# Delta rule's second pass: copies behind their updates, GpSimd's product at the head of a step, and the feed-forward branch shifted between the passes

## The chip, the cores and the metric

The kernel runs on one core of one Trainium2 chip. The metric is the device time of one execution in microseconds (us). The engines of the core work side by side, each through its own queue in program order: PE (TensorE, matrix products into PSUM), DVE (VectorE), ACT (ScalarE), POOL (GpSimd) and SP, which issues transfers.

## What is computed

The reference is a network of four layers on 4 x 1024 tokens of width 128, all in fp32; each layer adds an attention branch and a feed-forward branch to the tokens. Only the fourth layer bears on the change. Its attention branch is a delta rule: for each of 16 heads a state S of 8 x 8 is carried along the 1024 tokens. Its other branch is a feed-forward layer with a sine.

```python
# attention branch (delta rule), per head
v_new = (v_t - k_t @ S) * b_t
S = S + outer(k_t, v_new)
o_t = q_t @ S

# other branch
hidden = x @ W1 + b1
imag = w_imag * sin(theta + hidden * 0.1)
act = relu(hidden + (cos(theta) * w_real + sin(theta) * w_imag) * imag * 0.1)
out = act @ W2 + b2
```

## The kernel before, in words

`_delta_rule` cuts the 1024 tokens of each head into CH = 32 chunks of N = 32 tokens and works on all chunks at once, so that one step is one token of every chunk. The 128 partitions hold 4 batches x 16 heads x 2 halves of the value columns. There are three stages.

1. **First pass** (L1981 to L1994, 32 steps): every chunk starts from unit and zero states (`sm`, `sn` in PSUM), and what comes out are the linear map and the offset of each chunk.
2. **Scan** (L2006 to L2018, 31 steps on DVE): chunk after chunk, the true state at each chunk's start.
3. **Second pass** (L2028 to L2043, 32 steps and one more for the last state): the recurrence is run again from the true states, and the outputs are formed. The chunks form two halves of 16 chunks, one in `sm`, one in `sn`; both are worked in every step.

In the second pass, `differ` (L1941 to L1951) does one half of a step: on DVE `pro` (state times key, L1941), `dd` (a sum over d, L1944), a subtraction (L1946) and `u` (L1951). PE then builds the new state in PSUM by two additions (L1927): an identity matrix times `hist`, which is a copy of the old state in SBUF, then minus `u`. The copy from PSUM to `hist` is ACT's (L1955). POOL multiplies a complete `hist` with the query (`dprod`, L2041), and DVE sums that product into the output (`dvo`, L2025).

The order on PE, DVE, ACT and POOL is the order in which the program issues the instructions (the layer is under a hand-written schedule). In the order before, a step i issues for half 0: `pro`, the copy to `hist` (which was due before `pro`'s update), `dd`, the subtraction, `u`; then `output(i-2)`; then the same for half 1; then POOL's product of the state that this step copied. So the product issued at the end of one step is summed in the middle of the next one. `hist` and `dprod` have two buffers each.

The other branch is the generator `_waves` (L2047). It has 32 items (8 stretches of 512 tokens x 4 blocks of hidden units), worked in a pipeline of parts that alternate:

- **part A**: `close` of item n-3 (DVE L2110, every fourth item), `leave` of item n-2 (PE L2106), `sine` of item n-1: a clamp on DVE (L2094), then the sine on ACT (L2095);
- **part B**: `rest` of item n-1 (DVE L2099, ACT L2100), `enter` of item n (PE L2083, three activations on ACT, L2085, L2087, L2088), `fold` of item n (POOL L2091).

The clamp of an item thus waits for the `fold` of the part B before. `_layer3` (L2187) interleaves the two: `_delta_rule` yields 32 times in the first pass (n = 0 to 31, at the end of each step), 31 times in the scan (n = 32 to 62) and twice in each step of the second pass (from n = 63 on: an odd n lies between the halves, behind `output`; an even n lies at the end of the step). At some of these yields one part of `_waves` is issued. L2205 says at which: every odd n in the first pass (16 parts), two of three in the scan (21 parts), and every odd n in the second pass (33 parts): one part in the middle of every step, A and B in turn.

After that `_delta_out` (L2123) normalises and projects the outputs.

Of the kernel before, what the change touches and what calls it, by code (L numbers as in the profile page):

```python
# [16 lines left out]
ALU = mybir.AluOpType  # L17
AX = mybir.AxisListType
# [202 lines left out]
def _bc(ap, axis, n):  # L221

    ap = ap.unsqueeze(axis)
    shape = list(ap.shape)
    shape[axis] = n
    return ap.to_broadcast(shape)
# [1592 lines left out]
def _delta_rule(k, s, wl):  # L1819
# [6 lines left out]
    nc = k.nc  # L1826
    CH = 32
    N = L // CH
# [9 lines left out]
    room = lambda t: s.room(t).rearrange("p (c v d) -> p c v d", v=4, d=8)  # L1838
# [83 lines left out]
    def add(st, w, u, own, first, last):  # L1922

        for n in (slice(0, 16), slice(16, CH)):
            n = slice(max(n.start, own.start), min(n.stop, own.stop))
            if n.start < n.stop:
                nc.tensor.matmul(part(st, n), w, u[:, n], start=first, stop=last)  # L1927

    def part(st, own):

        if isinstance(st, list):
            half = own.start // 16
            return st[half][:, own.start - 16 * half : own.stop - 16 * half]
        return st[:, own]

    def differ(st, now, i, own, values):

        pro = room("pro")  # L1940
        nc.vector.tensor_tensor(pro[:, own], part(st, own), _bc(kp[:, i, own], 2, 4), ALU.mult)  # L1941
        add(st, k.ident, now(), own, True, False)
        d = turn()
        nc.vector.tensor_reduce(d[:, own], pro[:, own], AX.X, ALU.add)  # L1944
        if values:
            nc.vector.tensor_tensor(d[:, own], d[:, own], vp[:, i, own], ALU.subtract)  # L1946
        update(st, d, i, own)

    def update(st, d, i, own, first=False):
        u = room("u")  # L1950
        nc.vector.tensor_tensor(u[:, own], _bc(d[:, own], 3, 8), _bc(kp[:, i, own], 2, 4), ALU.mult)  # L1951
        add(st, k.neg_ident, u, own, first, True)

    def copy(now, st, own):
        nc.scalar.copy(flat(now[:, own]), flat(part(st, own)))  # L1955
        return now

    def states(t):
        return s.st_ps.tile([P, L], F32, name=t).rearrange("p (c v d) -> p c v d", v=4, d=8)
# [43 lines left out]
    st = [states(t) for t in ("sm", "sn")]  # L2003
# [15 lines left out]
    oc = ip.tile([P, N, CH, 4], F32, name="dvo")  # L2019
    q_at = qraw.rearrange("p d (c i) -> p c d i", i=N)  # L2020
    both_halves = slice(0, CH // 2), slice(CH // 2, CH)
    prod = None

    def output(i):
        nc.vector.tensor_reduce(oc[:, i], prod, AX.X, ALU.add)  # L2025


    for i in range(N + 1):  # L2028
        hist = room("hist")
        for half, own in enumerate(both_halves):  # L2030
            if i < N:
                differ(st, lambda: copy(hist, st, own), i, own, True)
            else:
                copy(hist, st, own)
            if half == 0 and i >= 2:
                output(i - 2)
            if half == 0:
                yield
        if i:
            prod = room("dprod")  # L2040
            nc.gpsimd.tensor_tensor(prod, hist, _bc(q_at[:, :, :, i - 1], 2, 4), ALU.mult)  # L2041
        yield
    output(N - 1)  # L2043
    s.oc, s.rq = oc, rq


# [140 lines left out]
def _layer3(k, s, a, out):  # L2187
    nc, tc = k.nc, k.tc
    wl = s.wl
    with ExitStack() as stack:  # L2190
        pool = lambda name, bufs, **kw: stack.enter_context(tc.tile_pool(name=name, bufs=bufs, **kw))
        stack.enter_context(tc.manual_schedule(engines=ENGINES3))
        s.ip = pool("di", 1)
        with ExitStack() as banks:
            s.dw, s.qw, s.qx = (
                banks.enter_context(tc.tile_pool(name=n, bufs=c)) for n, c in (("dw", 2), ("qw", 1), ("qx", 3))
            )
            bufs = {"hist": 2, "dprod": 2, "pro": 2, "u": 2}
            s.room = lambda n: s.dw.tile([P, L], F32, name=n, bufs=bufs[n])
            bank = lambda name, bufs: banks.enter_context(tc.tile_pool(name=name, bufs=bufs, space=PSUM))  # L2200
            s.st_ps, s.q_ps, s.q_out = bank("st_ps", 1), bank("q_ps", 2), bank("qo_ps", 1)
            s.d_ps = bank("d_ps", 1)
            waves = _waves(k, a, s)
            for n, _ in enumerate(_delta_rule(k, s, wl)):
                if n % 3 if 32 <= n < 63 else n % 2:  # L2205
                    next(waves, None)
            for _ in waves:
                pass
        _delta_out(k, s, wl, out)
# [4 lines left out]
def kernel(ctx: ExitStack, tc: tile.TileContext, a, out, at, where):  # L2214
# [55 lines left out]
    s = _weights3(k, a, ctx)  # L2270
    _layer2(k, a)
    _layer3(k, s, a, out)


# [15 lines left out]
```

## Time and profile before

| What | Value |
|---|---|
| median of three runs | 4741.51 us (4738.85 to 4744.04) |
| the profiled execution's own time | 4741.99 us |
| its span (first to last instruction) | 4740.2 us |
| mean granted TensorE clock | 0.859 |
| busy share of the span: PE, DVE, ACT, POOL | 83%, 65%, 54%, 14% |
| first pass: from the first to the last of its 32 `pro` of `sm` (L1941) | 4095.4 to 4347.2 us |
| scan: from the first to the last of its 31 additions (L2017) | 4363.9 to 4441.2 us |
| second pass: from the end of the scan to the end of the last `dvo` (L2025) | 4441.4 to 4689.0 us |

The times in a view are microseconds from the start of the span. A line of groups has the program line, the engine, the operation, the tiles (out<-in), the shapes and the count; then busy us and the mean ns of one; then the idle time of the engine just before and what ended it. A line of the timeline has start, duration, engine, line, operation and tiles, and in brackets the idle time before it with what ended it. The layers before the fourth one fill the first 3.9 ms and are not touched.

### The profile page before, as it was taken

Reading aid. Unit: us, or ns where it says so; the run is one execution under the profiler, and the core shown is the slowest. Engines: PE = TensorE matmul, PEld = TensorE weight load, DVE = VectorE, ACT = ScalarE, POOL = GpSimd, SP = SyncE. Lnnn points to the kernel's source line nnn. Section 1 sums busy time; section 2 is a strip of 40 time slices with the busy share of each in tenths; the row PEclk is TensorE's granted clock in tenths of the full one; section 3 lists DMA queues with packets and bytes.
Section 4 is the critical chain, followed back from the end, with each engine's and each line's share of the span. In section 5 each row is a group of like instructions: output and inputs, shape, how many; then the busy total and the mean of one; then the engine's idle time right before and its main releaser. Section 6 shows DMA issues by size and latency. Waiting matters only on the chain. (4 is left out here: it accounts for less than half of the span.)

```text
span 4740.2 us, 54727 instructions
## 1 busy us (share of the span) xinstructions
PE 3911.8 (83%) x21048; PEld 1791.9 (38%) x21048; DVE 3093.1 (65%) x4481; ACT 2583.1 (54%) x3674; POOL 685.3 (14%) x632
## 2 busy tenths in 40 slices
PE   4679999998968888888886888888879986898675
PEld 3223333364422222222223555555544463343221
DVE  5868989722335655656567888888565323799686
ACT  1257877831249999999993555555422222343332
POOL 2310000003200000000003223233103213000242
PEclk6689999999977777767777999999889997999688
DMA  2411111021221010010002111111100122400001
GB/s 87 119 41 56 29 56 29 11 70 50 15 83 58 18 50 18 27 36 18 18 1 78 34 36 41 36 37 34 51 1 20 52 72 67 109 1 9 0 0 53
DMA packets 107496, 191.83 MB, mean 40 GB/s; under 512 B 23138, under 2 KB 48354, under 8 KB 105378
## 3 DMA queue, kind: packets, MB, share of 16 engines
q1 hardware_dynamic: 98756, 166.31, 12.4%
q0 software_dynamic: 8192, 16.79, 1.7%
q10 hardware_dynamic: 288, 5.24, 0.3%
q8 instruction: 166, 2.72, 0.2%
q14 instruction: 94, 0.77, 0.1%
HBM read 95.00 MB, written 67.39 MB: 34 GB/s over the span
## 5 line engine op out<-in xcount | busy, mean ns | idle before, releaser
L790 DVE TENSOR_TENSOR p<-p,e 128x1024 f32<-128x1024 f32 x512 | 586.4, 1219 | 322.0 <-ACT e L788 322.0
L773 PE MATMUL big<-q,k 32*128 32x512 f32 x2048 | 559.3, 631 | 181.8 <-ACT p L784 76.7
L583 DVE TENSOR_REDUCE m<-mx 128x2 f32<-128x1024 f32 x512 | 620.9, 1223 | 101.2 <-PE mx L575 94.1
L468 PE MATMUL av<-p,v 128*32 128x256 f32 (+1 forms) x5632 | 666.3, 528 | 0.2
L666 ACT ACTIVATE p<-s 128x512 f32<-128x512 f32 x1024 | 551.1, 597 | 187.9 <-PE s L657 174.4
L773 PEld LDWEIGHTS big<-q,k 32*128 32x128 f32 x2048 | 210.0, 228 | 706.4 <-ACT e L788 351.1
L657 PE MATMUL s<-q,k 64*128 64x512 f32 x1024 | 278.6, 496 | 45.7 <-DMA q<-mrows 31.3
L788 ACT ACTIVATE e<-big,neg_mu 128x1024 f32<-128x1024 f32 x256 | 262.2, 1126 | 12.5 <-PE big L773 12.3
L575 PE MATMUL mx<-k,q 64*128 64x512 f32 x1024 | 239.4, 438 | 32.4 <-DVE m L583 17.8
L784 ACT ACTIVATE p<-big,neg_mu 128x1024 f32<-128x1024 f32 x256 | 261.3, 1201 | 2.5 <-PE big L773 2.3
L788 ACT ACTIVATE e<-big 128x1024 f32<-128x1024 f32 x256 | 242.6, 1040 | 27.5 <-PE big L773 25.9
L784 ACT ACTIVATE p<-big 128x1024 f32<-128x1024 f32 x256 | 239.4, 1072 | 8.4 <-PE big L773 8.1
L1227 POOL TENSOR_TENSOR lqk<-lt 128x512 f32<-128x512 f32 x128 | 162.7, 1271 | 516.5 <-DVE lt L1218 450.3
L1081 POOL DMA_INDIRECT cl_row<-res,back x128 | 122.3, 955 | 727.8 <-DMA in_l_su_sb<-in_l_su 473.5
L1200 PE MATMUL lps<-f_wqkv,lh 128*128 128x512 f32 x384 | 215.4, 649 | 11.0 <-DVE lo L1355 6.8
L468 PEld LDWEIGHTS av<-p,v 128*32 128x32 f32 x5632 | 121.3, 111 | 254.8 <-issue 205.2
L657 PEld LDWEIGHTS s<-q,k 64*128 64x128 f32 x1024 | 107.9, 184 | 284.2 <-issue 161.1
L1318 ACT ACTIVATE lsm<-lsm 128x512 f32<-128x512 f32 x128 | 80.6, 630 | 222.0 <-DVE lsm L1317 220.5
L1000 POOL DMA_INDIRECT buf<-xtok,to x128 | 129.0, 1008 | 402.5 <-DMA buf<-xtok,to 222.5
L1193 POOL MEMSET lva<- 128x32 f32 x16 | 2.4, 152 | 1147.0 <-PE av L468 1147.0
L1049 DVE TENSOR_TENSOR h<-h,up 128x640 f32<-128x640 f32 x64 | 52.6, 821 | 159.9 <-PE up L1046 80.7
L575 PEld LDWEIGHTS mx<-k,q 64*128 64x128 f32 x1024 | 108.5, 195 | 62.9 <-DVE m L583 46.8
(427 smaller groups left out, 7043.3 us busy)
## 6 DMA issues: line engine op xcount, KB each, us to landing
hl<-phi SPq DMA_DIRECT2D x64, 256.0 KB
hl<-plo SPq DMA_DIRECT2D x64, 256.0 KB
lvs<-lva SPq DMA_DIRECT2D x16, 520.0 KB
q<-hl SPq DMA_DIRECT2D x32, 256.0 KB
k<-hl SPq DMA_DIRECT2D x32, 256.0 KB
q<-hl SPq DMA_DIRECT2D x16, 512.0 KB
k<-hl SPq DMA_DIRECT2D x16, 512.0 KB
lvs<-lva SPq DMA_DIRECT2D x16, 390.0 KB
```

What stands on the lines that cost most here:

```text
L468: k.nc.tensor.matmul(av[32 * j : 32 * j + 32, cols], v[:, kc, 9 * (4 * g + j) : 9 * (4 * g + j) + 32], pts[j][:, cols], start=kc == 0, sto ...
L575: nc.tensor.matmul(ps[:, i, :], q[rows, gg, qt * P : (qt + 1) * P], key[rows, gg, half * W : (half + 1) * W], start=True, stop=True, tile_ ...
L583: nc.vector.tensor_reduce(m[:, qt, gg, :, half], ps, AX.X, ALU.max)
L657: nc.tensor.matmul(ps, key[rows, half, kc * P : (kc + 1) * P], q[rows, half, qh * W : (qh + 1) * W], start=True, stop=True, tile_position= ...
L666: nc.scalar.activation(p, ps, AF.Exp, scale=8.0**-0.5)
L773: nc.tensor.matmul(ps[:, jj, :], key[rows, kc * P : (kc + 1) * P], q[rows, qh * W : (qh + 1) * W], start=True, stop=True, tile_position=(3 ...
L784: nc.scalar.activation(p, ps, f, bias=bias, scale=scale)
L788: nc.scalar.activation(e, ps, f, bias=bias, scale=scale)
L790: nc.vector.tensor_tensor(p, p, e, ALU.mult)
L1000: nc.gpsimd.indirect_dma_start(out=buf, out_offset=bass.IndirectOffsetOnAxis(ap=to[:, t : t + 1], axis=0), in_=xtok[:, t, :], in_offset=None,)
L1200: nc.tensor.matmul(ps, z.h[:, t * P : (t + 1) * P], wqkv[:, own], start=True, stop=True)
L1227: nc.gpsimd.tensor_tensor(z.qk[t][:, own], r[0], r[1], ALU.add)
```

## The change

The second pass is rewritten. The first states are copied to `hist` ahead of the loop. In each step, the copy of a half's new state (into `ahead`) is issued right behind that half's update, and not behind the next step's `pro`. POOL's product of the previous state is issued at the head of the step, ahead of its DVE work, and `output(i-2)` in the middle of a step sums the product issued at the head of the step before, so that two products can be outstanding (`prods`). The extra step for the last state falls away; the last product and the last two outputs follow the loop. The loop yields 64 times and not 66.

The parts of the other branch are issued at other yields: in the first pass at every fourth (8 parts), in the scan at every other one (15), in the second pass at three of four (47): n = 63 and from then on all n that are no multiples of 4. Each step still has one part between its halves, and every other step has a second one at its end.

```diff
-    prod = None
+    prods = {}
+
+    def product(i, hist):
+        prods[i] = room("dprod")
+        nc.gpsimd.tensor_tensor(prods[i], hist, _bc(q_at[:, :, :, i], 2, 4), ALU.mult)
 
     def output(i):
-        nc.vector.tensor_reduce(oc[:, i], prod, AX.X, ALU.add)
-
-
-    for i in range(N + 1):
-        hist = room("hist")
+        nc.vector.tensor_reduce(oc[:, i], prods.pop(i), AX.X, ALU.add)
+
+
+    hist = room("hist")
+    for own in both_halves:
+        copy(hist, st, own)
+    for i in range(N):
+        ahead = room("hist")
+        if i:
+            product(i - 1, hist)
         for half, own in enumerate(both_halves):
-            if i < N:
-                differ(st, lambda: copy(hist, st, own), i, own, True)
-            else:
-                copy(hist, st, own)
-            if half == 0 and i >= 2:
-                output(i - 2)
+            differ(st, lambda: hist, i, own, True)
+            copy(ahead, st, own)
             if half == 0:
+                if i >= 2:
+                    output(i - 2)
                 yield
-        if i:
-            prod = room("dprod")
-            nc.gpsimd.tensor_tensor(prod, hist, _bc(q_at[:, :, :, i - 1], 2, 4), ALU.mult)
+        hist = ahead
         yield
-    output(N - 1)
+    product(N - 1, hist)
+    for i in (N - 2, N - 1):
+        output(i)
     s.oc, s.rq = oc, rq
...
             for n, _ in enumerate(_delta_rule(k, s, wl)):
-                if n % 3 if 32 <= n < 63 else n % 2:
+                if n % 4 == 3 if n < 32 else n % 2 if n < 63 else n % 4:
                     next(waves, None)
```

## The prediction

> **What bounds the kernel now.** I read the windows by stage, then the groups of the second pass, then its timeline, and last the places of the trace in which DVE and POOL meet. Windows (first pass, scan, second pass; busy us of each engine, then the granted clock):
>
> ```profile
> 4094.00:4357.00 263.00, 249.98 (x665) 113.71 (x664) 243.81 (x262) 98.11 (x120) 8.88 (x7) 0.99 0.06 13
> 4357.00:4444.00 87.00, 38.31 (x44) 11.71 (x42) 56.82 (x149) 37.06 (x55) 13.59 (x11) 0.58 0.03 7
> 4444.00:4689.00 245.00, 179.76 (x315) 62.73 (x314) 197.22 (x322) 83.83 (x138) 108.95 (x47) 0.88 0.00 0
> ```
>
> DVE (third figure behind the length) paces all three: full in the first pass, idle for 30 us in the scan and for 48 us in the second pass. The groups of the second pass name that idle time:
>
> ```profile
> L2041 POOL TENSOR_TENSOR dprod<-hist,raw 128x1024 f32<-128x1024 f32 x32 | 91.4, 2857 | 58.2 <-ACT hist L1955 58.2
> L2025 DVE TENSOR_REDUCE dvo<-dprod 128x128 f32<-128x1024 f32 x32 | 38.8, 1214 | 36.1 <-POOL dprod L2041 36.1
> L2094 DVE TENSOR_SCALAR qarg<-qarg 128x512 f32<-128x512 f32 x15 | 6.3, 418 | 3.9 <-POOL qarg L2091 3.9
> ```
>
> The output sum waits 36.1 us for POOL's product. The timeline shows how:
>
> ```profile
> 4493.67 0.73 DVE L2099 SCALAR_TENSOR_TENSOR qhid<-qarg,q_coef,qh 128x512 f32<-128x512 f32 x1
> ...
> 4496.53 0.72 ACT L2088 ACTIVATE qtmp<-qtmp,q_round 128x512 f32<-128x512 f32 x1
> ...
> 4497.15 0.57 ACT L1955 COPY hist<-sn 128x512 f32<-128x512 f32 x1
> 4497.32 1.27 POOL L2091 TENSOR_TENSOR qarg<-qarg,qtmp 128x512 f32<-128x512 f32 x1 [5.17 <-ACT qtmp L2088]
> ...
> 4498.55 2.85 POOL L2041 TENSOR_TENSOR dprod<-hist,raw 128x1024 f32<-128x1024 f32 x1
> ...
> 4501.44 1.22 DVE L2025 TENSOR_REDUCE dvo<-dprod 128x128 f32<-128x1024 f32 x1 [2.38 <-POOL dprod L2041]
> 4502.57 0.74 DVE L2110 SCALAR_TENSOR_TENSOR x<-qo,in_vecs_sb,x 128x512 f32<-128x512 f32 x1
> ...
> 4503.23 0.41 DVE L2094 TENSOR_SCALAR qarg<-qarg 128x512 f32<-128x512 f32 x1
> ```
>
> Call T the start of `rest` (L2099). The fold runs T+3.65 to T+4.92, the product starts 0.04 before the fold's recorded end, the output starts at T+7.77. The clamp (L2094) comes behind the output, when POOL is idle. It always does: its 32 durations are 415 to 427 ns.
>
> From DVE's starts I take pitches: half a step 2.33 (0.72 + 0.73 + 0.27 + 0.61), output 1.12, `rest` 0.66, clamp 0.33, `close` 0.66. Check on two steps of before: T+7.77, then 1.12 + 0.33 + 2.33 + 2.33 + 1.12 = 7.23, together 15.0; the pairs without `close` take 15.0 (6.43 + 8.58 between `pro` of `sm`).
>
> **First pass: 16 parts become 8.** A clamp there costs its step 0.33, a `rest` 0.65, both 0.98 with `close` (steps of 7.44 become 7.77, 8.09, 8.42). Steps 10 to 18, with the query norms, take 8.44, or 9.30 with a matmul of the branch (0.86 more). Taking away four clamps, four `rest`, a `close` and most matmuls of those steps, I sum the steps to 246.3 for 251.75 measured: **-5.4**.
>
> **Scan: 21 parts become 15.** From `rest` to clamp it takes 5.01 (4391.15 to 4396.16): three activations and the fold. Before, one scan step (1.40) lies between, and DVE waits 2.9 nine times or so; three steps take 8.03. After, two steps lie between: the wait is 5.01 - 0.66 - 2.80 = 1.55, seven times. First to last addition: 30 x 1.40 + 7 x (0.66 + 0.33 + 1.55) + 0.33 = 60.1, before 77.2: **-17.1**.
>
> **Second pass, the copies.** A copy ends 1.83 after `u` (PE 1.13, ACT 0.59, semaphores), about 2.6 at half clock (1.91 for 1.13). New is that `pro` of the next step waits for the copy[...] (in the first pass `pro` waits for ACT's copy). Between `u` and that `pro` lie the other half and the output, 3.45 at least, so it costs nothing; without that cover it would be up to 1.9 a half. On ACT the copy stands ahead of `relu` of a part B: priced below. The product at the head of a step removes the 36.1 but for the last product's 2.9; the tail behind the last `u` is 6.4.
>
> **Second pass, 33 parts become 47.** Four steps now hold three items: 4 x 5.78 + 3 x 0.99 = 26.1 of DVE work. Clamps and folds come in three positions, which repeat seven times (21 clamps in 28 steps).
>
> *a. B at the end of a step, A in the middle of the next.* On ACT the copy of the half just updated (to T+1.9) precedes `relu`, so the fold ends at T+6.0, not T+4.92. DVE arrives at T+0.66 + 2.33 + 1.12 = T+4.11: a wait of 1.9.
> *b. B in the middle, A at the end of the same step.* Arrival T+2.99, fold's end T+4.92: a wait of 2.0.
> *c. B in the middle, A in the middle of the next step.* Arrival T+6.44: no wait for the fold.
>
> So far 30.0 for four steps, the same 7.5 a step as before, with half as much again of the branch in it. But the clamp now stands beside the product. What happens when a DVE tensor_scalar between SBUF tiles meets a POOL tensor_tensor is in the trace, earlier in the kernel:
>
> ```profile
> 3418.73 1.31 POOL L1481 TENSOR_TENSOR x<-x,lt 128x512 f32<-128x512 f32 x1 [12.54 <-DVE lt L1476]
> ...
> 3418.95 1.17 DVE L2182 TENSOR_SCALAR pair<-pair 128x128 f32<-128x128 f32 x1
> 3420.04 0.68 DVE L287 TENSOR_TENSOR xn<-x,misc 128x512 f32<-128x512 f32 x1
> ```
>
> A quarter of the clamp's elements took 1.17 and ended 0.09 behind POOL's instruction; DVE's next one waited as well. Another (L1244) takes 0.48 in the one case of 16 beside POOL, 0.195 otherwise. The Trainium skill ("SBUF — State Buffer", section "SBUF: two separate sides") has the rule, and it speaks against this change: DVE in a two-port mode and GpSimd share a port pair as an exclusive lock; whoever starts first holds it for the whole instruction, the other stands still. 418 ns for 512 elements (the other DVE lines take 680 to 695) is such a mode, I infer. DVE's other lines here have at most one SBUF input and don't change beside POOL (`u` 692 ns either way), so only clamps pay. By the durations alone a clamp costs 0.33; by the rule and L2182 it stands until POOL ends, less some 0.13.
>
> *c:* the product starts 1.96 behind the step's start and ends at 4.82; the clamp arrives at 3.45 and gets through at 4.69: **1.24**; 1.85 if the fold is 0.6 late. I take 1.6.
> *a:* the product stands behind the fold in POOL's queue, ready since T+1.9. It starts at T+5.96; the clamp, 0.04 behind the fold's end, could start at T+6.04. First come wins: a DVE instruction 0.05 behind a POOL start was held (603 instead of 192 ns):
>
> ```profile
> 1328.56 1.73 POOL L274 COPY ln_s<-inv 128x512 f32<-128x512 f32 x3 [70.19 <-DVE inv L356]
> 1328.61 0.60 DVE L380 TENSOR_TENSOR ln_r<-var,inv 128x32 f32<-128x32 f32 x1 [0.17 <-DVE inv L356]
> ```
>
> So the clamp stands to T+8.69: **4.6** in place of 1.9. No row has this very pair; if the clamp wins, it is 1.9.
> *b:* the product needs the copy of the second half: `u` ends T+3.07, copy T+4.88, product T+4.94; the clamp is due at T+4.97. Nearly a tie. But PE idles some 4.7 in *a*; behind 3.11 of idle its pairs of matmuls already take 1.9 to 2.1 for 1.1. Then `copy`, and `relu` behind it, come up to 1.8 late, the copy is done ahead of the fold's end, and POOL goes from fold to product as in *a*. Bounds: 2.0 (clamp first, no delay) to 6.4 (4.6 + 1.8); I take **5.2**, POOL first with 0.6 of delay.
>
> Four steps: 26.1 + 1.6 + 4.6 + 5.2 = 37.5; seven times 262.5. The first step 5.3, the last three 18.0 with a `close` (the others hide in waits), tail 6.4: 292.2. Before: 4441.4 to 4689.0, 247.6. **+44.6.**
>
> No DMA is moved; SP has none here. Sum: -5.4 - 17.1 + 44.6 = +22. The profiled execution took 4741.99 (span 4740.2 and 1.8 around it), 0.5 above the median of 4741.51; the difference is put on the median: **4764**. With all waits at their ends but POOL first in *a* and *b*: 4750 to 4778.
>
> **Rivals.**
> 1. *Clamp first in b.* Waits 1.6 + 4.6 + 2.9 (0.9 late): 35.2; second pass 276; +6: 4748. For it: the near tie. Against: any delay of `relu` tips it.
> 2. *The lock holds only where the product is already under way (c).* This ends on the other side. In *a* and *b* the clamp is let in behind the fold: 26.1 + 1.2 + 1.9 + 2.0 = 31.2, second pass 248.5; -22: 4720. It decides at 0.08 between the product's start and the clamp's; the row with 0.05 is against it, though POOL's recorded starts may not be when it takes the port.
> 3. *No lock for the clamp.* 30.0 and two bare `close`: second pass 241, -29: 4712. L2182 and L1244 speak against it.
> 4. *Worse:* a part's late activations also hold the copies until `pro` waits: beyond 4784.
>
> **How the numbers follow.** Forecast 0.60, rival 1 0.14, rival 2 0.11, rival 3 0.09, rival 4 0.06. The range 4714 to 4784 takes in all but rivals 3 and 4. 0.2% (9.5 us) is about what a measurement of this kernel can tell from no change. Faster: rivals 2 and 3 and a little, 0.22. Same: half of rival 1, the forecast's edge: 0.12. Slower: 0.66.
>
> **What would show it.** Clamps of the second pass (L2094) far above 418 ns: near 3.0 in *a* and *b*, 1.6 in *c*; if all stay at 0.42, rival 3; if only *c* is long, rival 2. The wait of `dvo` for `dprod` should fall from 36.1 to about 3. First to last scan addition about 60. If second-pass DVE idles on `hist` or `sn`, my cover for the copies was wrong.

## The result and the profile after

The changed kernel takes 4777.41 us (median of four runs, 4775.79 to 4781.84), the kernel before 4742.77 in the same series (4738.85 to 4747.32): a ratio of 1.0074, with a 95% interval of 1.0057 to 1.0092. It is 34.6 us slower; the forecast was 22.

The windows by stage of the changed kernel (first pass, scan, second pass; length, then busy us of PE, its weight loads, DVE, ACT and POOL, the granted clock):

```profile
4101.00:4348.00 247.00, 234.45 (x628) 107.02 (x628) 229.76 (x244) 83.11 (x97) 3.80 (x3) 0.99 0.06 12
4348.00:4424.00 76.00, 35.87 (x52) 11.98 (x52) 63.26 (x153) 30.39 (x45) 10.11 (x8) 0.67 0.06 14
4424.00:4728.00 304.00, 202.15 (x342) 71.01 (x342) 255.98 (x338) 105.92 (x171) 117.15 (x53) 0.84 0.00 0
```

In the last row DVE counts 256 us as busy where it had 197 before. Only 8 us of the difference are work moved in from the other stages (seven `rest`, seven clamps and two `close` more, by the prediction's pitches). The rest is one group. Its row, by line, with the shortest, the median and the longest duration in ns, before and after:

```profile
L2094 DVE TENSOR_SCALAR qarg<-qarg x32: 415/418/427, 4145.3 to 4654.6; 128x512 f32<-128x512 f32 x32
```

```profile
L2101 DVE TENSOR_SCALAR qarg<-qarg x32: 415/2552/3067, 4197.2 to 4693.7; 128x512 f32<-128x512 f32 x32
```

The same clamp, the same 512 elements, now up to 3.07 us. No clamp of the first pass or the scan is long (415 to 427 ns); all 21 of the second pass are. The timeline of one step shows position *b* of the prediction (part B in the middle of a step, clamp at its end), and behind it, at 4513.32, position *c*:

```profile
4494.69 0.73 DVE L2106 SCALAR_TENSOR_TENSOR qhid<-qarg,q_coef,qh 128x512 f32<-128x512 f32 x1
...
4498.53 1.27 POOL L2098 TENSOR_TENSOR qarg<-qarg,qtmp 128x512 f32<-128x512 f32 x1 [1.61 <-ACT qtmp L2095]
4498.96 0.58 ACT L1955 COPY hist<-sn 128x512 f32<-128x512 f32 x1 [0.51 <-PE sn L1927]
4499.75 2.85 POOL L2026 TENSOR_TENSOR dprod<-hist,raw 128x1024 f32<-128x1024 f32 x1
4499.83 3.06 DVE L2101 TENSOR_SCALAR qarg<-qarg 128x512 f32<-128x512 f32 x1 [2.08 <-POOL qarg L2098]
...
4507.21 0.59 ACT L1955 COPY hist<-sm 128x512 f32<-128x512 f32 x1 [3.66 <-PE sm L1927]
4507.69 0.72 ACT L2107 ACTIVATE qhid<-qhid,in_vecs_sb 128x512 f32<-128x512 f32 x1
...
4511.80 2.85 POOL L2026 TENSOR_TENSOR dprod<-hist,raw 128x1024 f32<-128x1024 f32 x1
...
4513.32 1.62 DVE L2101 TENSOR_SCALAR qarg<-qarg 128x512 f32<-128x512 f32 x1
```

The fold ends at 4499.80. POOL goes straight on to the product, 4499.75; the clamp, released by the fold, is recorded from 4499.83 and ends at 4502.89, 0.29 behind the product's recorded end. The second clamp starts in the middle of a product and again ends 0.29 behind it. A clamp that stands is recorded as busy, not as idle; a reader of the waits alone sees only this, for the second pass of the changed kernel:

```profile
DVE qarg L2101 <- POOL qarg L2098: 37.7, 15, 3.4
DVE dvo L2029 <- POOL dprod L2026: 3.6, 1, 3.6
```

The wait for the product fell from 36.1 us to 3.6, and a wait for the fold of 37.7 came in its place (3.9 before). Beside these stand 50.7 us that are in no row of waits: the 21 clamps' durations less 0.418 each. The second pass thus has 32.5 less waiting for the product, 33.8 more for the fold, 50.7 of standing and 8 of moved work; `pro`'s 3.1 of waiting for PE went too. That makes 57 for the 55.7 measured (next paragraph).

Stage by stage, for the profiled executions: first pass (first to last `pro` of `sm`) 251.8 before and 245.5 after; scan (first to last addition) 77.2 and 59.2; second pass (end of the scan to the end of the last `dvo`) 247.6 and 303.3. That is -6.2, -18.0 and +55.7, together +31.5. The profiled execution of after took 4781.84 us, 39.9 more than that of before (4741.99). Of the other 8.4 us, 6.7 came ahead of the first pass (it began at 4102.1 in place of 4095.4), in layers whose code is the same, and 1.7 behind the second pass. In the third series below, three kernels whose code ahead of it is the same but for one small memset began the first pass at 4074.7, 4076.9 and 4080.2; I don't count this part as the change's.

### The profile page after: what moved, and what is told of

It is laid out like the page before. It is cut to its first block, busy times and chain, and to the rows that moved or that the text cites. A ratio compares the mean times of both kernels' runs of the same rounds, so it can differ in the third digit from the quotient of the medians.

```text
span 4780.1 us, 54688 instructions
## 1 busy us (share of the span) xinstructions
PE 3924.0 (82%) x21048; PEld 1797.4 (38%) x21048; DVE 3142.6 (66%) x4481; ACT 2582.3 (54%) x3674; POOL 685.2 (14%) x632
## 5 line engine op out<-in xcount | busy, mean ns | idle before, releaser
L773 PE MATMUL big<-q,k 32*128 32x512 f32 x2048 | 558.6, 631 | 182.0 <-ACT p L784 77.2
L1200 PE MATMUL lps<-f_wqkv,lh 128*128 128x512 f32 x384 | 216.7, 653 | 11.1 <-DVE lo L1355 6.8
L1927 PE MATMUL sm<-hist,in_const_sb 128*128 128x512 f32 x192 | 106.1, 666 | 42.5 <-DVE pro L1941 42.5
```

What stands on the lines that cost most here:

```text
L773: nc.tensor.matmul(ps[:, jj, :], key[rows, kc * P : (kc + 1) * P], q[rows, qh * W : (qh + 1) * W], start=True, stop=True, tile_position=(3 ...
L1200: nc.tensor.matmul(ps, z.h[:, t * P : (t + 1) * P], wqkv[:, own], start=True, stop=True)
```

## The experiments

Three explanations were to be told apart: the theory (DVE's clamp and POOL's product exclude each other at the port, whoever starts first holds it); density alone (47 parts in the second pass cost their own latency, whatever POOL does); and the copies (each copy behind its update holds up the next step). The port is the prediction's reading: what runs can show is whether the two instructions exclude each other.

The runs were made in three series, each with runs of the kernel before between them, on the same chip in a series: 4722.13 us in the first, 4745.02 in the second, 4723.33 in the third. A time is compared with its own series alone. The table has the stages from the profile.

| Kernel | median, us | beside before | ratio (95% interval) | first pass | scan | second pass |
|---|---|---|---|---|---|---|
| before | 4742.77 | | | 251.8 | 77.2 | 247.6 |
| after | 4777.41 | +34.6 | 1.0074 (1.0057 to 1.0092) | 245.5 | 59.2 | 303.3 |
| order_alone | 4710.39 | -11.7 | 0.9974 (0.9964 to 0.9983) | 252.4 | 77.2 | 232.6 |
| parts_alone | 4733.99 | +11.9 | 1.0026 (1.0015 to 1.0037) | 245.5 | 59.3 | 285.3 |
| clamp_psum | 4701.98 | -20.2 | 0.9953 (0.9937 to 0.9970) | 246.2 | 61.3 | 250.7 |
| clamp_pool | 4654.75 | -67.4 | 0.9857 (0.9841 to 0.9874) | 244.9 | 47.7 | 214.2 |
| product_ahead | 4749.52 | +4.5 | 1.0015 (1.0005 to 1.0025) | 245.6 | 59.3 | 271.2 |
| product_halves | 4745.79 | +0.8 | 0.9996 (0.9986 to 1.0006) | 245.6 | 59.2 | 267.1 |
| before_clamp_psum | 4729.03 | +5.7 | 1.0010 (1.0001 to 1.0020) | 253.5 | 79.9 | 250.8 |
| before_clamp_pool | 4714.16 | -9.2 | 0.9978 (0.9968 to 0.9987) | 250.4 | 61.7 | 252.4 |
| order_clamp_pool | 4667.62 | -55.7 | 0.9879 (0.9862 to 0.9895) | 251.1 | 61.7 | 206.8 |

### The two parts of the change, each alone

order_alone is the changed kernel with the yields of before:

```diff
-                if n % 4 == 3 if n < 32 else n % 2 if n < 63 else n % 4:
+                if n % 3 if 32 <= n < 63 else n % 2:
```

> The changed second pass (copies behind their updates, product at the head of a step) with the parts of the other branch at the yields of before (16, 21 and 33). Theory (the clamp stands still while GpSimd's product runs): one part a step, always between the halves, so only the clamp that meets a product already under way pays, some 1.25 us on each of 14 clamps, clamps of about 1.65 us; the 36 us of waiting for the product goes. Second pass about 221 us (before 247.6), in all about 4717. Rival A (the clamp pays nothing beside the product and the loss of the changed kernel is the denser parts' own latency): clamps of 0.42, second pass about 205, in all about 4702. Rival B (the copies behind their updates hold up the next step): second pass no shorter than before, 4740 or more.

It is faster than before by 11.7 us (some 24 were expected), so the copies behind their updates and the earlier product are a gain by themselves; rival B falls. Rival A falls by the clamps: from the ninth step of the second pass on, two steps take 13.77 (before 15.0), and the clamp in their middle is recorded with 1.66, or 1.00 where a `close` delays its start, always beside a product. Lines of such a step, POOL and DVE:

```profile
4525.04 2.86 POOL L2026 TENSOR_TENSOR dprod<-hist,raw 128x1024 f32<-128x1024 f32 x1
4525.40 1.21 DVE L2029 TENSOR_REDUCE dvo<-dprod 128x128 f32<-128x1024 f32 x1
...
4526.52 1.66 DVE L2101 TENSOR_SCALAR qarg<-qarg 128x512 f32<-128x512 f32 x1
```

The clamp comes 1.48 behind the product's start and gets through at its end: 1.24 over its 0.42, the size that was worked out for *c*. The output sum in the second row also reads SBUF and writes SBUF, and it runs inside the product undisturbed: 25 of the 32 do, in 1207 to 1214 ns, and the others take 1207 to 1220. So it is not every DVE instruction in SBUF that stands; the clamp is the one that does. The second pass is 11.6 above the 221 expected. Its first clamp met no product; the next three took 3.06, 3.06 and 2.34, with a wait of 2.2 ahead of the first of these, behind pairs of matmuls that took 1.90 to 2.05 for 1.02 (the granted clock was 0.50 at the scan's end). That is about 6 of it; the rest is small terms that I did not follow.

parts_alone is the kernel before with the yields of the change, the same line the other way round.

> The second pass of before with the parts at the yields of the change (8, 15 and 47). Theory: first pass and scan give back 24 us; in the second pass of before, the product stands ahead of a part at the end of a step, so a clamp in the middle of the next step meets no product, and only a clamp at the end of a step (7 of them) is held, about 2.6 us each; waits for fold and product stay. Four steps 34 to 36, second pass 268 to 280, in all 4740 to 4752. Rival A (density alone makes the loss, whatever the order of the product): the second pass near the 303 of the changed kernel, in all 4775 or more.

It gave back 24.2 us in first pass and scan, as expected, and lost 37.7 in the second pass, where 20 to 32 were expected; so it is 11.9 slower than before, a miss by a few us. But it is 18 short of the changed kernel's second pass, so density alone is not the whole loss. In which position a clamp is long answers to the theory: in *b* all seven take 3.06 or 3.07 (the product of the step stands behind the fold in POOL's queue), in *a* and *c* all thirteen 0.42 to 0.43, where the output sum, which needs the product, stands ahead of the clamp in DVE's queue. The waits are 29.5 us on the fold and 21.3 on the product, at the upper end of what the expected 34 to 36 us for four steps leave for them (37 to 51); the 5 us beyond the expectation I did not follow.

### The same fold, another clamp

clamp_psum leaves every instruction in its place and gives the clamp another form, with an operand in PSUM (which takes one of the four places of the sum `dd`):

```diff
     dd = s.d_ps.tile([P, 4, CH, 4], F32, name="dd")
-    turns = itertools.cycle(range(4))
+    s.floor = dd[:, 3, 0, 0:1]
+    nc.vector.memset(s.floor, -0.5)
+    turns = itertools.cycle(range(3))
...
-        nc.vector.tensor_scalar(z.arg, z.arg, 0.5, -0.5, ALU.min, ALU.max)
+        nc.vector.scalar_tensor_tensor(z.arg, z.arg, 0.5, s.floor.to_broadcast([P, W]), ALU.min, ALU.max)
```

> The changed kernel with the clamp as a scalar_tensor_tensor whose second operand is a constant in PSUM (in the sum's tile, of which three places and not four are then in turn): one SBUF input, no fast mode, some 0.74 us for 0.42. The fold's latency and the place of the clamp are as in the changed kernel. Theory: every clamp takes about 0.74 beside the product too, the 50 us that clamps stood beside products go, 7 us of longer clamps come; second pass 250 to 260, in all 4725 to 4735. Rival A (the long clamps are a wait for the fold or for GpSimd's queue, not the port): clamps stay at 3 us in the recording or the wait moves in front of them, second pass 295 or more.

This is the run that decides. All 32 clamps take 676 to 690 ns. The 21 of the second pass still run beside a product, and 12 of them still start 0.07 or 0.08 behind one:

```profile
4498.81 2.86 POOL L2028 TENSOR_TENSOR dprod<-hist,raw 128x1024 f32<-128x1024 f32 x1
4498.89 0.69 DVE L2103 SCALAR_TENSOR_TENSOR qarg<-qarg,dd 128x512 f32<-128x512 f32 x1 [2.92 <-POOL qarg L2100]
```

The second pass fell from 303.3 to 250.7, that is by 52.6: the 50.7 that clamps stood, and 7.6 less waiting for the fold (30.1 for 37.7), less 21 times the 0.26 that this form takes longer. The wait for the fold, 2.92 in the second row, is still there. The total beat its expectation: 20 us below before, where 7 to 17 were due. The form differs from the clamp's in two things, the instruction and the operand in PSUM; which of the two frees it the runs don't tell. The same form in the kernel before is the control:

> The kernel before with the clamp that reads a constant in PSUM (some 0.68 us for 0.42), as a control of that form: in the kernel before no clamp meets a product. Theory (what the form saved in the changed kernel is the time that clamps stood beside products): here it saves nothing and costs its 0.26 on some 32 clamps, 5 to 9 us more than the kernel before. Rival (the form helps by something else, the three places of the sum or the order): faster than before by 10 us or more.

It cost 5.7 us, as expected, so the form brings nothing where no clamp meets a product.

### Who comes first, and for how long

product_ahead issues the product at the end of a step, ahead of the part there:

```diff
-        if i:
-            product(i - 1, hist)
...
+        product(i, ahead)
         hist = ahead
         yield
-    product(N - 1, hist)
```

> The changed kernel with the product issued at the end of a step, ahead of the part there, and not at the head of the next (the same order on every engine but GpSimd, where product and fold change places when a part B ends a step). Theory: in position a (B at the end of a step, clamp in the middle of the next) the product has run before the fold, so the 7 clamps there take 0.42 in place of 3.06 and wait for the fold alone; b and c stay. 7 x 2.6 = 18 us less in the second pass: about 285, in all about 4759. Rival (what holds the clamp is not who comes first at the port): no clamp changes, or all do; 4777 or below 4740.

In *a*, all seven clamps take 0.43 and wait for the fold alone. In *b* four still take 3.06 and three do not, which I had not expected. The timeline at one of each:

```profile
4454.37 2.85 POOL L2026 TENSOR_TENSOR dprod<-hist,raw 128x1024 f32<-128x1024 f32 x1
4454.45 3.06 DVE L2099 TENSOR_SCALAR qarg<-qarg 128x512 f32<-128x512 f32 x1 [2.55 <-POOL qarg L2096]
...
4490.23 0.43 DVE L2099 TENSOR_SCALAR qarg<-qarg 128x512 f32<-128x512 f32 x1 [1.89 <-POOL qarg L2096]
4490.27 3.10 POOL L2026 TENSOR_TENSOR dprod<-hist,raw 128x1024 f32<-128x1024 f32 x1
```

At 4454 POOL is 0.08 ahead and the clamp stands. At 4490 the clamp is 0.04 ahead; it takes its 0.43, and now the product takes 3.10 in place of 2.85. This is the near tie of *b*, seen from its other side: here the fold ended at T+4.92, with no delay, and the copy that the product needs ended only 0.06 ahead of the fold (4490.14), so that the product started 0.07 behind the fold's recorded end and not 0.05 ahead of it, as at 4454. The gain over the changed kernel's second pass is 32 us, 18 of it in *a* as expected.

product_halves splits the product, so that each of its instructions takes half as long:

```diff
-        nc.gpsimd.tensor_tensor(prods[i], hist, _bc(q_at[:, :, :, i], 2, 4), ALU.mult)
+        for own in both_halves:
+            nc.gpsimd.tensor_tensor(
+                prods[i][:, own], hist[:, own], _bc(q_at[:, own, :, i], 2, 4), ALU.mult
+            )
```

> The changed kernel with each product in two instructions, one for each half of the chunks, some 1.43 us each. Theory: a held clamp gets in behind the instruction that is running, so the 14 clamps that start 0.08 behind a product take about 1.7 in place of 3.06, and those that meet a running one 0.4 to 1.7. 14 x 1.35 + 6 x 0.9 = 24 us less: second pass about 279, in all about 4753. Rival (the clamp waits for the whole product, as for a semaphore): 3.06 stays, no gain.

```profile
4563.43 3.18 POOL L2027 TENSOR_TENSOR dprod<-hist,raw 128x512 f32<-128x512 f32 x2
4563.51 1.72 DVE L2104 TENSOR_SCALAR qarg<-qarg 128x512 f32<-128x512 f32 x1 [2.42 <-POOL qarg L2101]
```

The 14 clamps of *a* and *b* all take 1.72 or 1.73, 1.30 over their own time in place of 2.64: half the hold, half the price. They get in between the two instructions, and the second one is recorded with 1.70 to 1.72 for it, where it takes 1.52 without a clamp. The second pass is 267.1, 36 below the changed kernel's, where 24 were expected; the shorter stops also shortened the waits for the fold, by some 9 us.

### No clamp on VectorE

clamp_pool is the changed kernel with the clamp behind the fold, on POOL, where it takes 0.61:

```diff
         nc.gpsimd.tensor_tensor(z.arg, z.arg, z.turns, ALU.subtract)
+        nc.gpsimd.tensor_scalar(z.arg, z.arg, 0.5, -0.5, ALU.min, ALU.max)
...
-        nc.vector.tensor_scalar(z.arg, z.arg, 0.5, -0.5, ALU.min, ALU.max)
```

> The changed kernel with the clamp on GpSimd, right behind the fold, and none on VectorE. Theory: no VectorE instruction of the second pass and the scan waits for the fold or meets GpSimd at the port any more; VectorE's own work is left (203 us in the second pass with the tail), the scan loses its waits of 1.55 too. Second pass 205 to 220, scan 45 to 50, in all 4665 to 4690. Rival (the branch's latency comes out elsewhere, as `rest` waiting for a sine that is later by GpSimd's clamp, or ScalarE's sine holding the copies): second pass 240 or more, in all 4705 or more.

Both the hold and the wait for the fold are gone from DVE, and the kernel is 67.4 us faster than before (ratio 0.9857); 29.6 us of that come from the scan, 33.4 from the second pass, as expected. The windows of scan and second pass:

```profile
4341.00:4389.00 48.00, 22.54 (x26) 7.21 (x26) 44.90 (x130) 22.94 (x34) 11.96 (x13) 0.61 0.00 0
4389.00:4604.00 215.00, 172.54 (x342) 60.16 (x342) 198.00 (x319) 107.44 (x173) 131.47 (x76) 0.95 0.00 0
```

DVE now is busy for 198 of 215 us with real work, where the changed kernel's 256 of 304 held 51 of standing. Whether this needs the change at all, two more kernels tell: the same move in the kernel before, and in order_alone.

> The kernel before with the clamp on GpSimd (0.61 us there), right behind the fold. Theory: in the second pass of before the product stands behind fold and clamp, so `dvo` waits 0.6 longer in 15 steps, less 0.33 of the clamp: 3 to 6 us more there; the scan loses VectorE's waits for the fold, and a part pair takes 6.3 to 6.5 for three steps in place of 8.03: 16 us less; first pass 4 less. In all 12 to 20 us below the kernel before. Rival (the clamp's place alone made the gain of clamp_pool, and the second pass's new order nothing): 60 us or more below.

> The changed second pass with the parts at the yields of before and the clamp on GpSimd. Theory: with no clamp on VectorE the new order gains its 36 us in full: second pass 200 to 210, scan 58 to 64, first pass 248 to 251; in all 52 to 64 us below the kernel before, a little above clamp_pool, whose denser second pass hides more of the branch. Rival (the gain of clamp_pool comes from the parts' new places): no more than 30 us below.

In the kernel before it brings 9.2 us, a little less than expected: 15.5 in the scan, 1.3 and not 4 in the first pass, and the second pass grows by 4.8, because the product waits behind the clamp too (`dvo` waits 45.3 for it, 36.1 without the move). With the new order it brings 55.7: a second pass of 206.8. So the order is worth 46 us once no clamp stands in its way, 12 with the clamp on DVE, and with the clamp on DVE and the parts at the change's places it is worth less than nothing (parts_alone 285.3, after 303.3). clamp_pool is the fastest of all kernels here.

## Why the prediction was right, and where its size was off

**First pass and scan.** Forecast -5.4 and -17.1, measured -6.2 and -18.0. The wait for the fold in the scan was put at 1.55; the trace has 1.57 to 1.58 five times and 0.94 twice, with a `close`.

**The copies.** Forecast at nothing, hidden by the other half and the output. No row of waits of the second pass has `pro` waiting for `hist`, so rival 4 falls, and order_alone, which has these copies, is faster than before. (In the trace of before no `pro` overlaps ACT's copy of the same PSUM tile in time.)

**The hold.** The step that carried the forecast: every clamp beside a product stands until POOL is done, less some 0.13. Forecast 3.07 long in *a* and *b*; all fourteen were 3.06. POOL's start lay 0.07 or 0.08 ahead of the clamp in each, as worked out for *a*. Rivals 2 and 3 fall with these rows, rival 1 too: in the changed kernel *b* went POOL's way seven times of seven. product_ahead shows that rival 1 was a real possibility, three times of seven there, where the fold was not late (T+4.92 each time); in the changed kernel the fold of *b* ended at T+5.1 to T+6.7, late every time, as forecast. The prediction's row with 0.05 (`ln_r`) was weaker support than it looked: that instruction has two inputs in SBUF and is not of the clamp's kind. The runs settle it for the clamp.

**The size.** The second pass was forecast at 292.2 and took 303.3. The terms, each with the wait ahead of the clamp and what the clamp took over 0.418:

- *a*: forecast 4.6, measured 2.46 + 2.64 = 5.10, seven times: 3.5 us. I had left `relu` free of PE's clock there; the fold ended T+5.9 in three cases and T+7.1 to T+7.4 in four, where the copy ahead of `relu` waited for matmuls at half clock.
- *b*: forecast 5.2, measured 2.70 + 2.64 = 5.33, seven times: 0.9 us.
- *c*: forecast 1.6, measured 1.85, six times: 1.5 us.
- the first clamp of the second pass: counted as a *c*; it waited 1.65 for a fold that ended T+6.99, and stood 2.65 behind a product that had got ahead of it: 2.7 us.

That is 8.6 of 11.1; the other 2.5 I can't place. The term that was mis-sized is the delay of the fold by a slow PE. It shows behind a clamp that stands, here for two additions to `sm`:

```profile
4498.76 1.02 PE L2113 MATMUL qo<-qhid,in_l_w_sb 128*128 128x512 f32 x2
4503.54 2.07 PE L1927 MATMUL sm<-hist,in_const_sb 128*128 128x512 f32 x2 [3.75 <-DVE pro L1941]
4505.40 1.71 PE L1927 MATMUL sm<-u,neg_ident 128*128 128x512 f32 x2
4506.95 1.02 PE L2090 MATMUL qh<-xn,in_l_w_sb 128*128 128x512 f32 x2
```

While the clamp stands, PE has nothing to do for 3.75; its next pairs take 2.07 and 1.71 for 1.02; the copy at 4507.21 is late by that, `relu` starts 1.44 behind `rest` in place of 0.77, and the next fold is late. A hold thus lengthens the next wait. That this feedback is real shows in clamp_psum and product_halves: with no hold or half of it, the fold of *a* ends at T+5.9 to T+6.0 in all seven cases, as the forecast had it. The second passes of product_halves and product_ahead gained 10 and 4 us more than their shorter or missing holds explain (26 of 36 and 28 of 32). The granted clock of the second pass fell from 0.88 to 0.84; that the clock is all of the feedback was not tried. Nor is idle time alone a sure sign of a slow PE: of the twelve gaps of 3.1 us in the second pass of before, ten had slow matmuls (0.8 to 1.22 each) among the next five, and two had five at full speed (0.59 to 0.70).

The forecast of +22 became +34.6. In the stages it is +31.5; the other 3 lie within what the layers ahead of the first pass differ from execution to execution.

## What to carry to other kernels

An instruction that is moved from behind a wait may have been protected by that wait. Here DVE's clamp came behind the sum that waits for POOL's product (13 of 15 times in the second pass; the first two came before any sum and met no product either), and so never met POOL; taking the wait away put it beside the product, and with the parts at their new places 36 us of waiting became 51 of standing (19 with the parts at the old ones, and there the new order was a gain). Before moving GpSimd's work, list the VectorE instructions that will now run beside it and whose duration is well below that of others of the same size, as the clamp's is, and those with two inputs in SBUF (the `ln_r` row of the prediction: 603 for 192 ns), and look in the trace for one place where such a pair meets: a duration that grows is the price, and no row of waits will show it.

## What was not expected of the hardware

- Hundredths of a microsecond decide: in all fourteen clamps of *a* and *b* POOL was 0.07 or 0.08 ahead and the clamp stood for the whole product, in three of product_ahead the clamp was 0.04 or 0.05 ahead and cost the product 0.25. The lead of POOL is the same to 0.01 us whenever the product follows the fold at once; when the product's copy was late, as at 4490 in product_ahead, the race fell the other way.
- GpSimd's clamp of 128x512 takes 0.61 and VectorE's alone 0.42; GpSimd's tensor_tensor of that size takes 1.27 (fold) and 1.5 (half a product). The clamp, with one input, was the cheap one to move; whether the second input makes the difference was not tried.
